# A side step that copies a convolution's or projection's result takes the next step into its unit, and a chunk's rows of B are loaded six units sooner

## The chip, the cores and the metric

The kernel runs on one core of one Trainium2 chip. The metric is the device time of one execution in microseconds (us). The engines are named as in the profile: PE is TensorE's matmul and PEld its weight load, DVE is VectorE, ACT is ScalarE, POOL is GpSimd, and SP is SyncE, which here only issues DMAs (SPq is its queue).

## The reference

Four layers are applied one after the other to an image batch x of shape (8, 48, 48, 96), each as x = x + ss2d(group_norm(x)). What one layer computes, cut to what matters:

```python
xc, z = split(x @ in_proj_w.T)                    # 192 channels each
xc = silu(depthwise_conv3x3(xc) + conv_b)
xs = [xc by rows, xc by columns, and both reversed]   # K = 4 ways through L = 2304 places
dts, Bs, Cs = split(einsum('bkdl,kcd->bkcl', xs, x_proj_w))   # rank, 16, 16 rows
delta = softplus(einsum('bkrl,kdr->bkdl', dts, dt_proj_w) + dt_bias)
def step(h, (u, dl, B, C)):                       # scan over l; h is (b, k, 192, 16)
    h = exp(dl * A) * h + (dl * u) * B
    y = sum over the 16 states of h * C
y = sum of the four ways, put back in place, + D * xs
return (layernorm(y) * silu(z)) @ out_proj_w.T
```

The fourth layer writes the same scan as cumulative sums.

## The kernel before, in words

The images are worked on in four pairs. For each layer and pair, the 192 channels of two images are three tiles t of 128 partitions (the first 128 channels of each image, and the last 64 of both). Each tile is scanned in two orders (ph, by rows or by columns) and two directions (d): 12 groups. A group is three chunks of 768 places, and a chunk has 16 units, n = 0 to 15, each of which holds two of the 16 states for 64 channels. So a pair has 12 x 3 x 16 = 576 units, and layers 0 to 2 have 12 pairs and 6912 units. (Layer 3 runs a short form, "Edge", which the change leaves as it is; a full form of layer 3 stands behind a condition.)

The order of all work is written out by hand: one Python loop in `run` issues unit after unit, and each engine then works through its own queue in that order. In iteration k, which scans unit k, the loop issues:

1. loads by SP (`get_ready`): `load_b` the rows of B, spread over 64 partitions, for the pooled unit k+5 (tile `bb`, line L740), `load` those of C for unit k+4 (tile `cb`, L740). At the first unit of a chunk `load` also loads `brow` (L765): the chunk's rows of B for all states, as three bf16 parts on 96 partitions, in two DMAs. It has two buffers. As `load` runs four units ahead, this is issued at n = 12 of the chunk before;
2. `spread` of unit k+1: for 10 of 16 units PE multiplies `brow` by a 0/1 matrix `pick` and so spreads two rows over a PSUM tile `b` (L678; two buffers). For the six pooled units (n = 2, 5, 7, 10, 13, 15) ACT writes the decay exp(dl*A) into such a tile instead (L780);
3. `weigh` of unit k+3 if pooled: POOL multiplies `bb` by du (L757), and `decay` by ACT (L780);
4. the carries (ACT, L698), and `scan`: DVE multiplies `b` by du (L810, not for pooled units) and scans (L814); POOL multiplies C by the result (L823);
5. one step of `prepare` for the next chunk (delta and delta * u; lines L614 to L645, L589);
6. one side step through `beside`, not at n = 3, 9 and 10 (`full`);
7. `add_up` of unit k-2: PE adds the products up over the states (L870);
8. at n = 12 and 14 (`free`) a second side step.

Side steps belong to two generators that run beside a pair: `behind`, the epilogue of the pair before (layernorm, gate, output projection, residual; L1031 to L1136), and `ahead`, the prologue of the pair that follows (group norm, in-projection L411 and L420 with copies L415 and L424, convolution L314 with its copy L322, x_projections L472 with copies L483 and L485, and the splitting of B into bf16 parts). For the first pair a third, `rest`, finishes its own prologue. `side_step` takes the side that holds a PSUM bank, or else the one that is less far along by `made / total`. Nearly every step is one visit to one engine: a yield of True says that a bank is filled and must be read next. Both the side steps and `prepare` take their banks from one pool `ps` of two PSUM buffers (`bank()`). A convolution's piece of 480 places is nine steps on PE and then one on ACT, the copy; an in-projection's is one on PE and one on ACT; an x_projection's two on PE and one on ACT. A prologue that waits for buffers of u yields GATED.

Of the kernel before, what the change touches and what calls it, by code (L numbers as in the profile page):

```python
# [40 lines left out]
BF16 = mybir.dt.bfloat16  # L41
# [62 lines left out]
def ss2d_layers_kernel(ctx: ExitStack, tc: tile.TileContext, x_in, consts, weights, out):  # L104
# [177 lines left out]

    GATED, READY = "gated", "ready"
    halves_of = [slice(64 * g, 64 * g + 64) for g in range(2)]

    def prologue(l, p, short=False, first=False):
# [14 lines left out]
        def convolve(pad, t):  # L303

            while place["tiles"] < t and not first:
                yield GATED
            u[t] = upool.tile([P, L], F32, name=f"u_{l}_{p}_{t}", tag="u")
            for c0, m in CHUNKS:
                r0, nr = c0 // W, m // W
                ps = bank()  # L310
                for j in range(9):
                    dy, dx = divmod(j, 3)
                    for half in halves_of:
                        nc.tensor.matmul(  # L314
                            ps[half, :m],
                            ly.diag[:, int(t == 2), j, half],
                            pad[:, r0 + dy : r0 + dy + nr, dx : dx + W],
                            start=(j == 0),
                            stop=(j == 8),
                        )  # L320
                    yield True
                nc.scalar.activation(  # L322
                    u[t][:, c0 : c0 + m], ps[:, :m], AF.Identity, bias=ly.column(t, C_CONVB)
                )
                yield
            silu(u[t], u[t])
            yield

# [5 lines left out]
        for b in range(2):  # L334
            x = tmp.tile([DM, L], F32, name=f"x_{l}_{p}_{b}", tag="tmp")
            if l == 0:
                loaded = []

                def load(c0, m):
                    ld = sm2.tile([P, 4, DM], F32, name="ld", tag="ld")  # L340
                    nc.sync.dma_start(
                        ld[: m // 4],
                        x_in[2 * p + b, c0 : c0 + m, :].rearrange("(q j) c -> q j c", j=4),
                    )
                    loaded.append(ld)

                load(*CHUNKS[0])
                load(*CHUNKS[1])
                for _ in range(3):
                    yield  # L350
                for i, (c0, m) in enumerate(CHUNKS):
                    q, ld = m // 4, loaded[i]
                    ps = bank()
                    for j in range(4):
                        nc.tensor.transpose(
                            ps[0:DM, j * q : (j + 1) * q], ld[:q, j, :], ident[:q, :q]
                        )
                    yield True
                    nc.scalar.copy(
                        x[:, c0 : c0 + m].rearrange("c (q j) -> c j q", j=4),  # L360
                        ps[0:DM, :m].rearrange("c (j q) -> c j q", j=4),
                    )
                    if i + 2 < NCH:
                        load(*CHUNKS[i + 2])
                    yield
            for c0, m in CHUNKS:
                piece = slice(c0, c0 + m)
                if l == 0:
                    nc.sync.dma_start(src[b, :, piece], x[:, piece])
                else:  # L370
                    nc.sync.dma_start(x[:, piece], src[b, :, piece])
                yield
            for _ in range(2):
                yield


            st = sm1.tile([DM, NCH, 6], F32, name="st", tag="st")
            for i, (c0, m) in enumerate(CHUNKS):
                nc.vector.bn_stats(st[:, i, :], x[:, c0 : c0 + m])
                if i % 2 == 1:  # L380
                    yield
            mv = sm1.tile([DM, 2], F32, name="mv", tag="mv")
            nc.vector.bn_aggr(mv, st.rearrange("p a b -> p (a b)"))
            yield
            ps = bank()
            nc.tensor.matmul(ps[0:DM, 0:1], minus_group, mv[:, 0:1], start=True, stop=True)
            yield True
            mg = sm1.tile([DM, 1], F32, name="mg", tag="mg")
            nc.scalar.copy(mg, ps[0:DM, 0:1])
            dv = sm1.tile([DM, 1], F32, name="dv", tag="dv")  # L390
            nc.scalar.activation(dv, mv[:, 0:1], AF.Square, bias=mg)
            nc.scalar.activation(dv, dv, AF.Identity, bias=mv[:, 1:2])
            yield
            ps = bank()
            nc.tensor.matmul(ps[0:DM, 0:1], group_w, dv, start=True, stop=True)
            yield True
            scale, shift = gn[:, b, 0:1], gn[:, b, 1:2]
            nc.scalar.activation(scale, ps[0:DM, 0:1], AF.Ln, bias=gn_eps[0:DM])
            nc.scalar.activation(scale, scale, AF.Exp, scale=-0.5)
            nc.scalar.activation(shift, mg, AF.Copy, scale=scale)  # L400
            nc.scalar.activation(x, x, AF.Identity, bias=shift, scale=scale)
            yield

            pad = padded(f"pad_{l}_{p}_{b}")
            q0 = 64 * b
            for c0, m in CHUNKS:
                r0, nr = c0 // W, m // W
                rows = slice(1 + r0, 1 + r0 + nr)
                ps = bank()
                for half in halves_of:  # L410
                    nc.tensor.matmul(  # L411
                        ps[half, :m], ly.inw[:, half], x[:, c0 : c0 + m], start=True, stop=True
                    )
                yield True
                nc.scalar.copy(  # L415
                    pad[:, rows, 1 : W + 1], ps[:, :m].rearrange("p (r w) -> p r w", w=W)
                )
                yield
                ps = bank()
                nc.tensor.matmul(  # L420
                    ps[q0 : q0 + 64, :m], ly.inw[:, P:DIN], x[:, c0 : c0 + m], start=True, stop=True
                )
                yield True
                nc.scalar.copy(  # L424
                    pad2[q0 : q0 + 64, rows, 1 : W + 1],
                    ps[q0 : q0 + 64, :m].rearrange("p (r w) -> p r w", w=W),
                )
                yield
            if not (first and b == 1):
                yield from convolve(pad, b)  # L430
        yield from convolve(pad2, 2)
# [42 lines left out]
        def x_projection(i, ph, b):  # L474
# [20 lines left out]
            for j, (c0, m) in enumerate(CHUNKS):  # L495
                later(o + 3 * j, True, mul, 0, c0, m)
                later(o + 3 * j + 1, True, mul, 1, c0, m)
                later(o + 3 * j + 2, False, lambda *a: put(got["ps"], *a), c0, m)
            def store(c0, m):
                nc.sync.dma_start(xd[ph, b, :, c0 : c0 + m], got["xt"][:, c0 : c0 + m])  # L500

# [48 lines left out]
        def x_projections(*which):  # L550
            for i, (ph, b) in enumerate(which):
                (x_projection_of_ends if short else x_projection)(i, ph, b)
            for i in range(max(steps) + 1):
                held = False
                for holds, f, args in steps.get(i, ()):
                    f(*args)
                    held = held or holds
                yield held
            steps.clear()

# [139 lines left out]
    class Chunk:  # L700
# [52 lines left out]
        def weigh(self, n):  # L753

            if self.pooled(n):
                b = self.b[n][:, : self.m]
                nc.gpsimd.tensor_mul(b, b, self.du[n % 2])  # L757

        def load(self, n):

            s, m, at = state[self.l, self.p], self.m, slice(self.c0, self.c0 + self.m)
            if n == 0:
                self.brow = rpool.tile([2 * NR, SCAN], BF16, name="brow", tag="brow")
                for j, b in enumerate(range(2) if self.t == 2 else (self.t, self.t)):
                    nc.sync.dma_start(  # L765
                        self.brow[NR * j : NR * j + NR, :m],
                        s["xb"][self.ph, b, :, self.d, :, at],
                    )
            self.cb[n] = cb = cbpool.tile([P, SCAN], F32, name="cb", tag="cb")
            self.fetch(cb, NS, n)  # L770

# [390 lines left out]
    def side_step(*sides):  # L1162

        for s in sorted(sides, key=lambda s: (not s.held, s.made / s.total)):
            got = next(s.g, s)
            s.held = got is True
            if got is not s and got is not GATED:
                s.made += 1
                return True
        return False  # L1170

    marks = []
# [20 lines left out]
    def run(pairs, short):  # L1193
# [58 lines left out]
        for k, ((l, p, unit), c, n) in enumerate(todo):  # L1252
# [15 lines left out]
            if n == max(0, per - 1 - DECAYS):  # L1268
                while coming_to < len(chunks) and not chunks[coming_to].ready:
                    next(coming)  # L1270
            if n == 10 and coming_to + 1 < len(chunks):
                z = chunks[coming_to + 1]
                if (z.l, z.p) == (l, p):
# [13 lines left out]

            def beside(some):
                for _ in range(some):
                    side_step(rest) or side_step(behind, ahead)  # L1290

            step(coming)
            if l not in short:
# [1 line left out]
            if k >= LAG:  # L1295
# [3 lines left out]
                sum_of(b, bn)  # L1299
                if k > LAG and todo[k - LAG - 1][0][:2] != (bl, bp):  # L1300
                    done = todo[k - LAG - 1][0][:2]
            beside(10 if l in short else n in free)
        for i in range(len(todo) - LAG, len(todo)):
            collected()
            sum_of(todo[i][1], todo[i][2])
# [113 lines left out]
```

## Time and profile before

| | us |
|---|---|
| median of 3 runs (lowest, highest) | 20198.45 (20187.92, 20203.4) |
| the profiled execution | 20189.92 |
| its span, first to last instruction | 20188.1 |
| mean granted TensorE clock in it | 0.913 of full speed |

The costliest groups of the profile (line, engine, operation, tiles and shapes, count, then busy us and mean ns of one, and behind the bar the idle time of the engine just before them with what ended most of it):

```profile
L823 POOL TENSOR_TENSOR cb<-cb,da 128x768 f32<-128x768 f32 x4320 | 7833.8, 1819 | 641.4 <-issue 128.5
L870 PE MATMUL acc<-cb,twin 128*64 128x384 f32 x27648 | 7063.6, 540 | 428.6 <-POOL cb L823 407.7
L814 DVE TENSOR_TENSOR_SCAN da<-da,carry,b 128x768 f32<-128x768 f32 x2880 | 5222.7, 1813 | 177.5 <-ACT carry L698 1.9
L810 DVE TENSOR_TENSOR b<-du,b 128x768 f32<-128x768 f32 x4320 | 4079.2, 944 | 679.1 <-PE b L678 667.7
L780 ACT ACTIVATE da<-dl,a 128x768 f32<-128x768 f32 x4320 | 4016.5, 931 | 440.8 <-POOL cb L823 408.7
```

From one L814 scan to the next, over the 6912 of the main stage, takes 2.62 us on average; a pair takes 1490.4 to 1532.9 us, and a chunk 39 to 49 us by its place in the pair.

### The profile page before, as it was taken

The page shows a single profiled execution, that of the slowest core. Times are in us where ns is not written, and L with a number is a line of the kernel's source. Part 1 is how long each engine was busy: PE and PEld are TensorE (multiplying, and loading weights), DVE is VectorE, ACT ScalarE, POOL GpSimd, SP SyncE. Part 2 cuts the span into 40 slices and gives each one's busy share as a digit, 9 for nine tenths or more (in the row PEclk, how much of TensorE's full clock was granted, in tenths as well). Part 3 has the DMA queues.
Part 4 walks back from the last instruction along what each step waited for, and adds up shares of the span by engine and source line. Part 5 has one row for each costly group of instructions (what it writes and reads, how often), then busy time and mean ns, then how long its engine had stood idle before and what let it go on. Part 6 is the DMA issues. An engine that isn't in the chain of part 4 may idle for free.

```text
span 20188.1 us, 315179 instructions
## 1 busy us (share of the span) xinstructions
PE 16706.7 (83%) x92962; PEld 7669.4 (38%) x92962; DVE 17650.0 (87%) x14161; ACT 16275.9 (81%) x30014; POOL 17759.8 (88%) x10121
## 2 busy tenths in 40 slices
PE   8887887887888888888887888888888887888886
PEld 3333333333333333333333333333333333334555
DVE  6999988998999999999999999999999999996553
ACT  6777887887887887887887887887887887887786
POOL 6999999999999999999999999999999999995442
PEclk9998998998998998998998998998998998999997
DMA  5888888888888898888888888888888888884221
GB/s 159 228 228 221 226 218 221 229 219 222 224 226 224 222 232 222 222 233 222 222 233 221 223 226 223 220 226 223 221 228 221 223 228 222 222 220 117 79 76 51
DMA packets 2021152, 4200.81 MB, mean 208 GB/s; under 512 B 375920, under 2 KB 789360, under 8 KB 2017904
## 3 DMA queue, kind: packets, MB, share of 16 engines
q1 hardware_dynamic: 2019440, 4180.55, 79.9%
q8 instruction: 762, 12.48, 0.3%
q14 instruction: 950, 7.78, 0.2%
HBM read 4026.64 MB, written 152.27 MB: 207 GB/s over the span
## 4 chain that ended last, share of the span: by engine, by line
PE 17%; ACT 16%; DMA 15%; DVE 14%; issue 9%; SPq 3%; POOL 2%; DVEq 0%; ACTq 0%; POOLq 0%
DVE da L814 7%; DMA cb<-xd 6%; DMA bb<-xd 5%; PE acc L870 4%; DVE b L810 4%; ACT b L780 3%; PE ps L634 2%; PE ps L314 2%; ACT dl L589 2%; ACT du L589 2%; ACT da L780 2%; SPq L740 2%; PE b L678 2%; DVE bb L814 2%; DMA brow<-xb 2%
## 5 line engine op out<-in xcount | busy, mean ns | idle before, releaser
L823 POOL TENSOR_TENSOR cb<-cb,da 128x768 f32<-128x768 f32 x4320 | 7833.8, 1819 | 641.4 <-issue 128.5
L870 PE MATMUL acc<-cb,twin 128*64 128x384 f32 x27648 | 7063.6, 540 | 428.6 <-POOL cb L823 407.7
L814 DVE TENSOR_TENSOR_SCAN da<-da,carry,b 128x768 f32<-128x768 f32 x2880 | 5222.7, 1813 | 177.5 <-ACT carry L698 1.9
L757 POOL TENSOR_TENSOR bb<-bb,du 128x768 f32<-128x768 f32 x2592 | 4715.9, 1819 | 386.3 <-DMA bb<-xd 221.1
L823 POOL TENSOR_TENSOR cb<-cb,bb 128x768 f32<-128x768 f32 x2592 | 4712.7, 1818 | 54.3 <-DVE bb L814 31.8
L810 DVE TENSOR_TENSOR b<-du,b 128x768 f32<-128x768 f32 x4320 | 4079.2, 944 | 679.1 <-PE b L678 667.7
L780 ACT ACTIVATE da<-dl,a 128x768 f32<-128x768 f32 x4320 | 4016.5, 931 | 440.8 <-POOL cb L823 408.7
L678 PE MATMUL b<-brow,pick 96*64 96x512 bf16 (+2 forms) x18816 | 2837.9, 349 | 1545.8 <-DVE da L814 1123.2
L870 PEld LDWEIGHTS acc<-cb,twin 128*64 128x64 f32 x27648 | 2355.2, 148 | 3536.3 <-issue 2177.9
L780 ACT ACTIVATE b<-dl,a 128x768 f32<-128x768 f32 x2592 | 2337.4, 902 | 1115.8 <-DVE da L814 1015.7
L814 DVE TENSOR_TENSOR_SCAN bb<-b,carry,bb 128x768 f32<-128x768 f32 x1728 | 3109.7, 1800 | 94.0 <-ACT b L780 66.8
L814 DVE TENSOR_TENSOR_SCAN da<-da,b 128x768 f32<-128x768 f32 x1440 | 2524.6, 1753 | 87.4 <-DVE b L810 0.9
L678 PEld LDWEIGHTS <-pick 96*64 96x64 bf16 x18816 | 1149.4, 116 | 3794.4 <-DVE da L814 2251.3
L314 PE MATMUL ps<-pad,diag 128*64 128x480 f32 (+1 forms) x8640 | 2169.2, 563 | 69.8 <-DVE eyc L1086 32.5
L589 ACT COPY du<-ps 64x384 f32<-64x384 f32 x3456 | 1635.7, 473 | 236.7 <-DVE ps L645 118.6
L589 ACT COPY dl<-ps 64x384 f32<-64x384 f32 x3456 | 1634.3, 473 | 212.3 <-PE ps L634 171.4
L634 PE MATMUL ps<-du,cst 128*64 128x384 f32 (+1 forms) x7296 | 1581.4, 501 | 259.4 <-ACT du L628 244.8
L814 DVE TENSOR_TENSOR_SCAN bb<-b,bb 128x768 f32<-128x768 f32 x864 | 1502.1, 1739 | 151.8 <-ACT b L780 108.8
L634 PE MATMUL ps<-dl,cst 128*64 128x384 f32 (+1 forms) x7296 | 1453.9, 486 | 0.0
L614 PE MATMUL ps<-dts,w 6*128 6x384 f32 (+5 forms) x2432 | 920.7, 578 | 391.2 <-ACT du L589 214.6
L314 PEld LDWEIGHTS ps<-pad,diag 128*64 128x64 f32 x8640 | 665.1, 138 | 769.6 <-issue 571.4
L634 PEld LDWEIGHTS ps<-du,cst 128*64 128x64 f32 x7296 | 621.1, 142 | 871.1 <-ACT du L628 452.9
(144 smaller groups left out, 19011.3 us busy)
## 6 DMA issues: line engine op xcount, KB each, us to landing
cb<-xd SPq DMA_DIRECT2D x13952, 192.0 KB
bb<-xd SPq DMA_DIRECT2D x5184, 192.0 KB
brow<-xb SPq DMA_DIRECT2D x864, 72.0 KB
ey<-yd SPq DMA_DIRECT2D x256, 216.0 KB
cb<-xd SPq DMA_DIRECT2D x128, 384.0 KB
yd<-y SPq DMA_DIRECT2D x216, 192.0 KB
ex<-xs SPq DMA_DIRECT2D x256, 108.0 KB
xb<-parts SPq DMA_DIRECT2D x96, 216.0 KB
```

The costliest lines, as they stand in the source:

```text
L314: nc.tensor.matmul(ps[half, :m], ly.diag[:, int(t == 2), j, half], pad[:, r0 + dy : r0 + dy + nr, dx : dx + W], start=(j == 0), stop=(j == 8),
L589: nc.scalar.copy(z[64 * h : 64 * h + 64, g, at], v[64 * g : 64 * g + 64])
L614: nc.tensor.matmul(o[:, :m], ly.dtw[q0 : q0 + r, k, chans], dts[q0 : q0 + r, at], start=True, stop=True,)
L634: nc.tensor.matmul(v[half], ident[:, half], z1, start=(i == 0), stop=(i == 3))
L678: nc.tensor.matmul(o[64 * h : 64 * h + 64], pick[:, b, n : n + 1].to_broadcast([2 * NR, 64]), rows, start=True, stop=True,)
L740: nc.sync.dma_start(o[64 * h : 64 * h + 64, : self.m], xd[self.ph, b, row : row + 1, self.c0 : self.c0 + self.m].to_broadcast([64, self.m]),)
L757: nc.gpsimd.tensor_mul(b, b, self.du[n % 2])
L780: nc.scalar.activation(da, self.dl[n % 2], AF.Exp, scale=layers[self.l].a2[:, int(self.t == 2), n % 2, k, i : i + 1],)
L810: nc.vector.tensor_mul(b, self.du[n % 2], b)
L814: nc.vector.tensor_tensor_scan(way(h), way(da), way(b), start, ALU.mult, ALU.add)
L823: nc.gpsimd.tensor_mul(c, c, h)
L870: nc.tensor.matmul(self.acc[64 * g : 64 * g + 64, a, : self.m // 2], twin, c[:, a, :], start=False, stop=(pair + 2 == NS and not self.turns),)
```

## The change

It has four edits, all of which act in the stage of layers 0 to 2:

- A step that copies a convolution's, in-projection's or x_projection's result out of its bank, with another piece to follow, yields MORE. `side_step` hands this on, and `beside` then makes one more side step in the same unit. That next step is chosen as any other is, so it may be the other generator's.
- The second side step at n = 12 and 14 is made only if `in_arrears()`: if the steps made of both sides lag behind the unit's share of their total, counted one chunk ahead.
- A step of `x_projections` that holds both a copy and other functions passes MORE on, unless one of them holds a bank.
- `brow` of the next chunk is loaded by a new `load_rows` at n = 6, ahead of that iteration's loads, if that chunk is of the same layer and pair; `load` at n = 0 of a chunk loads it only where this was not done.

```diff
-                yield
+                yield MORE if c0 + m < L else None          # convolve, after the copy
...
-                yield
+                yield MORE                                  # in-projection, first copy
...
-                yield
+                yield MORE if c0 + m < L else None          # in-projection, second copy
...
-                later(o + 3 * j + 2, False, lambda *a: put(got["ps"], *a), c0, m)
+                later(
+                    o + 3 * j + 2, MORE if j + 1 < NCH else False,
+                    lambda *a: put(got["ps"], *a), c0, m,
+                )
...
-                    held = held or holds
+                    held = True if held is True else holds or held
...
+        def load_rows(self):
+            if self.brow is not None:
+                return
+            self.brow = rpool.tile([2 * NR, SCAN], BF16, name="brow", tag="brow")
+            for j, b in enumerate(range(2) if self.t == 2 else (self.t, self.t)):
+                nc.sync.dma_start(
+                    self.brow[NR * j : NR * j + NR, : self.m],
+                    state[self.l, self.p]["xb"][
+                        self.ph, b, :, self.d, :, self.c0 : self.c0 + self.m
+                    ],
+                )
...
             if n == 0:
-                self.brow = rpool.tile([2 * NR, SCAN], BF16, name="brow", tag="brow")
...
+                self.load_rows()
...
-                return True
+                return MORE if got is MORE else True        # side_step
...
+            if n == 6 and coming_to < len(chunks):
+                z = chunks[coming_to]
+                if (z.l, z.p) == (l, p) and l not in short:
+                    z.load_rows()
...
             def beside(some):
                 for _ in range(some):
-                    side_step(rest) or side_step(behind, ahead)
+                    if (side_step(rest) or side_step(behind, ahead)) is MORE and l not in short:
+                        side_step(rest) or side_step(behind, ahead)
+
+            def in_arrears():
+                made, total = behind.made + ahead.made, behind.total + ahead.total
+                return made * all_units < total * (unit + NS)
...
-            beside(10 if l in short else n in free)
+            beside(10 if l in short else n in free and in_arrears())
```

More of the change, by code (lines that the diff above doesn't have):

```diff
@@ L281, in ss2d_layers_kernel @@
     place = {"tiles": 3}
-    GATED, READY = "gated", "ready"
+    GATED, READY, MORE = "gated", "ready", "more"
     halves_of = [slice(64 * g, 64 * g + 64) for g in range(2)]
@@ L757, in weigh @@
                 nc.gpsimd.tensor_mul(b, b, self.du[n % 2])
+        def load_rows(self):
[9 more added lines that the diff above has]
+                )
         def load(self, n):
-            s, m, at = state[self.l, self.p], self.m, slice(self.c0, self.c0 + self.m)
             if n == 0:
-                self.brow = rpool.tile([2 * NR, SCAN], BF16, name="brow", tag="brow")
[L764 to L768, printed above, removed]
+                self.load_rows()
             self.cb[n] = cb = cbpool.tile([P, SCAN], F32, name="cb", tag="cb")
```

## The prediction

> **What bounds the kernel now.** I read the page's busy shares first, then one table of windows, then the waits of each engine, and last the timeline at one chunk's edge.
>
> ```profile
> PE 16706.7 (83%) x92962; PEld 7669.4 (38%) x92962; DVE 17650.0 (87%) x14161; ACT 16275.9 (81%) x30014; POOL 17759.8 (88%) x10121
> ```
>
> ```profile
> 171.90:18292.40 18120.50, 15031.71 (x81614) 6533.92 (x81614) 16738.18 (x12599) 14767.95 (x27219) 17043.80 (x9679) 0.91 0.87 224
> 18292.40:20188.10 1895.70, 1551.98 (x10816) 1088.04 (x10816) 901.15 (x1539) 1434.45 (x2667) 710.11 (x425) 0.90 0.26 72
> ```
>
> The first line is the busy time of each engine. The two others are windows: the scan stage of layers 0 to 2 (its columns are PE, PEld, DVE, ACT, POOL, clock, DMA share, GB/s), and the rest. The diff touches the first alone, apart from one wording that changes nothing in the rest. There POOL works 17043.80 of 18120.50 us, DVE 16738.18, and the DMA engines 0.87. So no engine is bound by itself: POOL's idle 1077 us is all that scheduling could ever give, and a delay on PE costs time only when DVE or POOL runs dry behind it. The waits say when that happens:
>
> ```profile
> PE b L678 <- DVE da L814: 1123.2, 1068, 4.3
> ...
> PE b L678 <- DMA brow<-xb: 284.4, 121, 7.5
> ...
> PE ps L420 <- ACT pad L415: 17.9, 19, 1.6
> ...
> DVE b L810 <- PE b L678: 667.7, 522, 12.4
> ...
> POOL bb L757 <- DMA bb<-xd: 221.1, 197, 5.0
> ...
> SPq L740 <- PE b L678: 1377.4, 1181, 7.9
> SPq L740 <- PE acc L870: 1352.8, 1108, 9.2
> ...
> SPq L740 <- DMA brow<-xb: 471.6, 488, 2.0
> ```
>
> Columns: total us, times, longest. PE, about to spread a chunk's first state over the partitions, waits 121 times for the chunk's rows of B (brow); DVE's largest wait is for those spreads. SyncE mostly waits for buffers, so it reaches its loads ahead of time. One edge, in the timeline (start us, duration, engine, in brackets the idle time before):
>
> ```profile
> 3003.74 1.55 SPq L765 DMA_DIRECT2D brow<-xb  x2
> ...
> 3006.64 1.17 SPq L740 DMA_DIRECT2D bb<-xd  x2
> ...
> 3011.04 0.52 PE L678 MATMUL b<-brow,pick 96*64 96x512 bf16 x4 [2.33 <-DMA brow<-xb]
> ...
> 3014.28 1.81 POOL L757 TENSOR_TENSOR bb<-bb,du 128x768 f32<-128x768 f32 x1 [1.35 <-DMA bb<-xd]
> ...
> 3016.67 0.96 DVE L810 TENSOR_TENSOR b<-du,b 128x768 f32<-128x768 f32 x1 [2.27 <-PE b L678]
> ```
>
> brow is issued at 3003.74 and ends PE's wait at 3011.04, 7.3 us later. Behind the waiting spread stand PE's side step and sums, so the next spread is late and DVE idles 2.27. The load of bb, issued just after brow, is late too.
>
> **Part 1, brow six units sooner.** From every brow issue to the scan it feeds I find a median of 10.2 us; in the waiting chunks, from issue to the end of PE's wait, 5.7 to 8.5 us (5th to 95th percentile; median 7.2). Six units of 2.62 us put 15.7 us in front: every such wait goes, except at a pair's first chunk, which is not moved (1 of the 121 waits). What a wait costs: from the scan two units before a chunk to the one four units after it, inside pairs, takes 17.0 us in the 120 chunks with it and 15.57 in the 300 without. Some of this is place, since waits crowd in certain chunks; with the chunk's place in its pair held fixed it is 1.02 us a chunk, or 0.64 us per us of PE's wait. So 120 x 1.02 = 122 us. Lower end: the extra POOL idle of those chunks, 0.63 x 120 = 76. Upper: 1.43 x 120 = 172. I take 122, as it compares like with like.
>
> A page of the Trainium skill speaks against there being anything to gain: "DMA: Bandwidth & Descriptors", Anatomy of one DMA, gives a fixed 2.0 us plus bytes at 436 GB/s (measured on the POOL path). An estimate from it for two loads of 72 KB is 2.3 us, so a load issued 10 us ahead would always be in time, this part would be worth 0, and the sum below would be -18 instead of -140. The trace's 7.2 us, with the DMA engines 0.87 busy, decides against it.
>
> brow's two DMAs are also moved on SP's queue: past six units of cb and bb loads and the load of dts. They take 2 x 0.74 us to issue, and SP waits 471.6 us in all for brow's semaphore. Before, the bb of unit n = 2 came next but one behind them. POOL's waits for a bb that end by that DMA are 119 us where unit 2 is weighed, 18 of them at pair starts, and 39 where unit 7 is. If unit 2 becomes like 7 in-pair, POOL gets 62; unit 13 now comes behind brow (two units behind, not one; its wait is 0.04 a chunk today), and I give it half of that. 31 left; the edges are those where PE waited too, so I count 25 (bounds: a loss of 30 if unit 13 takes it all and more, a gain of 80).
>
> **Part 2, the copy and the next step in one unit, and the second step of n = 12 and 14 only in arrears.** The instructions are the same ones; their place changes. Counted over the 12 pairs: 6024 side steps before, 6014 after (the rest is drained at pair ends); units 12 and 14 with two steps fall from 797 to 301; 552 steps follow a copy in its unit (216 the copy of an in-projection, 188 of an x_projection, 148 of a convolution); 204 of the 552 are the epilogue's step, as the side less far along is taken. Nothing is added to PE, ACT or DVE, so the price is only waits.
>
> Gain: fewer doubled units just before a chunk's edge. In the 300 in-pair chunks without a brow wait, DVE still waits 28 + 110 + 60 = 198 us for spreads at n = 0, 1 and 3. If a quarter of that comes of the doubled units, of which 62% go: 198 x 0.25 x 0.62 = 31. Bounds 0 and 123 (all of it).
>
> Loss: the two banks of `ps`. A step that starts in the copy's own unit finds its bank just being read, and PE's in-order queue (behind it the sums L870 and the next spread, for which DVE waits) stands until ACT has copied. In the instruction streams, of 1495 starts of a bank by a side step, 471 wait for an ACT instruction issued in the same unit; after, 704: 233 more. Nearest row: PE L420 on the copy L415, 17.9 us in 19 waits; about 35 of those starts wait for the copy in their own unit, so 0.51 us each. 233 x 0.51 = 119 us on PE; at most the 0.64 of part 1 reaches the end, 76; a sum stands between and pooled units need no spread, so half: 38. Bounds: 0 (the wait falls where PE waits for DVE anyway, the 1123 us row) and 76.
>
> "Perfetto Trace Analysis", Matmuls, says that independent groups should rotate over PSUM banks so that one's evacuation overlaps the next one's matmuls. Taken alone it speaks against this part: with every added same-unit wait at the full 0.94 us of the L420 row and all on the path, the term would be 219 and the sum a loss of 41.
>
> **Sum.** -122 - 25 - 31 + 38 = -140 us. The profiled execution took 20189.92 (span 20188.1), the median of three is 20198.45, 8.5 above it. 20198.45 - 140 = 20058. With all bounds at their best: -172 - 80 - 123 = -375; at their worst: -76 + 30 + 76 = +30. About 0.2%, 40 us, is what a measurement of this kernel can tell from no change.
>
> **Rivals.**
> 1. Same: the wait moves. PE's next limit at the edge is the release of a spread's buffer (1123 us, 1068 times), and only POOL's 76 us come free, less the loss of 38 to 76: 0 to -38, some 20180. For it: POOL and DVE are both within 8% of full, so freed time on one meets the other. Against: both idle at the same edges.
> 2. Slower: PE stands behind ACT. Place: the 552 followed copies. ACT is 81% busy and its copy queues behind exps of 0.93 us, so a follower may wait a whole copy. Price: at the 0.94 us of the L420 row and 0.64 to the path, 552 x 0.94 x 0.64 = 332, less the 178 gained: +154, 20352. It decides from 0.50 us per follower. For: in-projection and x_projection stretches get up to 18 to 20 steps a chunk instead of 15. Against: L472's and L314's waits for their copies today are a few us in all.
> 3. More gain: the edges' waits hang together, and brow, bb and the remaining spreads go at once: -375 + 38 = -337, 19861.
> 4. The load is not sooner in fact: SP stands at that place for buffers. SP's waits are 1.2 us on average, against 15.7; I give it no share of its own.
>
> **How the numbers follow.** Forecast (-140, its own range 19960 to 20160): 0.55. Rival 3: 0.12. Rival 1, within 40 us: 0.13. Rival 2: 0.20. So faster 0.67, same 0.13, slower 0.20. The range runs from 19900, inside rival 3, to 20250, into the mild half of rival 2; about 0.05 is left out below, 0.14 above.
>
> **What would show it.** PE's wait for brow falls from 284 us to under 30 (pair starts), POOL's for bb from 221 to under 180; DVE's wait L810 for the spread from 668 to about 500; SP's wait for brow stays. PE's waits for the copies (the L420, L472, L314 and first epilogue rows) grow by about 120. The stage 171.90:18292.40 shortens by 140, the tail by nothing. I am wrong if brow's wait is gone and DVE's wait for PE is not smaller (rival 1 or 2), and rival 2 holds if those copy rows grow by over 270.

## The result, and the profile after

The changed kernel takes 20304.74 us, the median of 6 runs (20279.07 to 20316.65), against 20200.93 for 6 runs of the kernel before (20187.92 to 20207.37): a ratio of 1.0051, 95% interval [1.0038, 1.0064]. It is slower by half a per cent, where 140 us less were forecast. The profiled execution took 20299.78 us, at a granted clock of 0.91 of full speed.

First the page: the busy time of each engine.

```profile
span 20297.8 us, 315609 instructions
PE 16716.1 (82%) x92962; PEld 7597.4 (37%) x92962; DVE 17657.5 (87%) x14161; ACT 16272.2 (80%) x30014; POOL 17764.8 (88%) x10121
```

Counts are those of before and no engine works more than 10 us longer, so the 110 us of longer span are all waiting. The windows of the scan stage and of what follows it (PE, PEld, DVE, ACT, POOL busy, clock, DMA share, GB/s):

```profile
172.06:18392.39 18220.33, 15030.23 (x81614) 6454.01 (x81614) 16745.23 (x12599) 14764.96 (x27219) 17048.76 (x9679) 0.91 0.86 223
18392.39:20297.80 1905.41, 1562.44 (x10816) 1095.76 (x10816) 901.60 (x1539) 1433.80 (x2667) 710.16 (x425) 0.89 0.25 71
```

The stage is 18220.33 - 18120.50 = 100 us longer, the rest 10. POOL's work in the stage is within 5 us of before (17048.76 against 17043.80); only its idle time grew. Now the waits (total us, times, longest):

```profile
PE b L682 <- DVE da L825: 1362.9, 1097, 4.3
...
DVE b L821 <- PE b L682: 707.0, 546, 14.1
...
POOL bb L761 <- DMA bb<-xd: 169.7, 125, 5.6
...
PE ps L421 <- ACT pad L416: 54.7, 38, 2.5
...
PE ps L473 <- ACT xt L486: 35.5, 20, 3.4
...
PE ps L315 <- ACT u L323: 33.2, 26, 1.9
...
PE ps L473 <- ACT xt L484: 27.0, 23, 1.7
```

```profile
SPq L744 <- PE acc L881: 1519.3, 1162, 8.0
...
SPq L744 <- DMA brow<-xb: 232.1, 281, 2.0
```

PE's wait for brow, 284.4 us before, no longer appears. In its place the wait for a free spread buffer grew from 1123.2 to 1362.9. DVE's wait for the spreads, the row that the forecast wanted to shrink to 500, is 707.0 against 667.7. And the four rows in which PE waits for a copy that may now be followed add up to 150.4 us, where before they were 33.5 (17.9, 6.7, 3.0 and 5.9, from the trace's records). The timeline shows one such place (start us, duration, engine; in brackets the idle time before):

```profile
4924.27 0.56 ACT L416 COPY pad<-ps 128x480 f32<-128x480 f32 x1
...
4924.88 0.78 PE L1042 MATMUL ps<-ey,centre 128*128 128x144 f32 x2 [1.52 <-ACT pad L416]
...
4927.03 1.52 PE L881 MATMUL acc<-cb,twin 128*64 128x384 f32 x4
...
4928.37 0.51 PE L682 MATMUL b<-brow,pick 96*64 96x512 bf16 x4
...
4928.92 0.96 DVE L821 TENSOR_TENSOR b<-du,b 128x768 f32<-128x768 f32 x1 [3.15 <-PE b L682]
```

This is iteration n = 6 of a chunk. ACT comes to the in-projection's copy late, the epilogue's step L1042 that follows it holds PE for 1.52 us, the sums and the spread of unit 8 stand behind it, and DVE idles 3.15 us. DVE's waits for spreads in the stage, summed by unit from the trace's records, show where this gathers (g1 and g2 are experiments below; us):

| spread of unit | 0 | 1 | 3 | 8 |
|---|---|---|---|---|
| before | 96 | 293 | 108 | 68 |
| early rows alone (e1) | 36 | 211 | 149 | 62 |
| after | 42 | 213 | 96 | 187 |
| after, followers of n = 6 behind the sums (g1) | 49 | 218 | 90 | 145 |
| after, all followers behind the sums (g2) | 33 | 222 | 101 | 122 |

The first two columns carry the gain of the early rows, the last a loss of 119 us. Unit 14, not in the table, goes the same way: 8 us before and in e1, 56 after. Of waits over 1.2 us at unit 8, 24 stand less than 5 us behind a PE wait of over 0.6 us for a copy of the followed kinds: 72 us in all. Before there are none.

### The profile page after: what moved, and what is told of

Read it like the earlier page. It is cut to its first block, busy times and chain, and to the rows that moved or that the text cites. A ratio compares the mean times of both kernels' runs of the same rounds, so it can differ in the third digit from the quotient of the medians.

```text
span 20297.8 us, 315609 instructions
## 1 busy us (share of the span) xinstructions
PE 16716.1 (82%) x92962; PEld 7597.4 (37%) x92962; DVE 17657.5 (87%) x14161; ACT 16272.2 (80%) x30014; POOL 17764.8 (88%) x10121
## 4 chain that ended last, share of the span: by engine, by line
ACT 23%; PE 22%; DVE 20%; DMA 16%; issue 14%; POOL 3%; SPq 3%; DVEq 0%; ACTq 0%; POOLq 0%
DVE da L825 10%; DMA cb<-xd 7%; DMA bb<-xd 6%; DVE b L821 6%; PE acc L881 5%; ACT b L791 4%; ACT dl L593 4%; ACT du L593 3%; PE ps L315 3%; ACT da L791 3%; PE ps L638 3%; DVE bb L825 2%; POOL cb L834 2%; PE b L682 2%; SPq L744 2%
## 5 line engine op out<-in xcount | busy, mean ns | idle before, releaser
L881 PE MATMUL acc<-cb,twin 128*64 128x384 f32 x27648 | 6915.3, 540 | 402.5 <-POOL cb L834 384.2
L821 DVE TENSOR_TENSOR b<-du,b 128x768 f32<-128x768 f32 x4320 | 4081.0, 945 | 722.8 <-PE b L682 707.0
L682 PE MATMUL b<-brow,pick 96*64 96x512 bf16 (+2 forms) x18816 | 2786.9, 349 | 1534.1 <-DVE da L825 1362.9
L881 PEld LDWEIGHTS acc<-cb,twin 128*64 128x64 f32 x27648 | 2285.7, 148 | 3534.7 <-issue 2279.9
L315 PEld LDWEIGHTS ps<-pad,diag 128*64 128x64 f32 x8640 | 622.7, 140 | 837.8 <-issue 554.9
```

What stands on the lines that cost most here:

```text
L315: nc.tensor.matmul(ps[half, :m], ly.diag[:, int(t == 2), j, half], pad[:, r0 + dy : r0 + dy + nr, dx : dx + W], start=(j == 0), stop=(j == 8),
L682: nc.tensor.matmul(o[64 * h : 64 * h + 64], pick[:, b, n : n + 1].to_broadcast([2 * NR, 64]), rows, start=True, stop=True,)
L821: nc.vector.tensor_mul(b, self.du[n % 2], b)
L881: nc.tensor.matmul(self.acc[64 * g : 64 * g + 64, a, : self.m // 2], twin, c[:, a, :], start=False, stop=(pair + 2 == NS and not self.turns),)
```

## The experiments

All are timed over five rounds beside the kernel before on the same chip; differences are against that chip's own median, which lay between 20163 and 20181. Three causes of loss are held against each other, where letters stand for them: W, PE's wait for the bank that is just being copied; D, a second step at a place in the chunk where PE has no room; P, the turn that all later steps are pushed into, so that they meet other units.

**The parts apart.** e1 keeps the early rows alone:

```diff
-                    if (side_step(rest) or side_step(behind, ahead)) is MORE and l not in short:
-                        side_step(rest) or side_step(behind, ahead)
+                    side_step(rest) or side_step(behind, ahead)
-            beside(10 if l in short else n in free and in_arrears())
+            beside(10 if l in short else n in free)
```

e2 is the change without the early rows (the block `if n == 6 ...: z.load_rows()` taken out). e3 is e2 with `n in free` again unconditional, so the followers alone. e4 is e2 without the follower, so the rule `in_arrears` alone.

> The early load of brow alone; the side steps as before. Theory A (the load gains as reckoned, and the followed copies cost more than that): 20200 less 76 to 172, so 20030 to 20125, and PE's wait for brow is gone. Theory B (PE's wait for brow was hidden: another wait takes its place, and the load is worth nothing): within 40 of 20200. Theory C (the load does the harm, by its place in SP's queue ahead of the cb and bb loads of the later half of the chunk): about 20300, with POOL's waits for bb or cb larger than before.

> The other part alone: the followed copies and the second steps of n = 12 and 14 only in arrears; brow is loaded as before. Theory A: 20380 to 20480, that is the changed kernel's 20304 and the load's gain on top. Theory B: about 20305, as the changed kernel. Theory C: about 20200 or below.

> The followed copies alone: second steps at n = 12 and 14 always, as before, brow as before. Theory A1 (a step that starts in its copy's unit holds PE): as slow as the two together, 20380 to 20480. Theory A2 (the loss comes of the second steps that are left out at n = 12 and 14, so that side work runs on longer): near 20200, and the fourth kernel of this set is the slow one.

> The rule of arrears alone: a second step at n = 12 and 14 only where the sides lag; no copy is followed, brow as before. Theory A1: 20170 to 20230, since the steps need nearly all slots without the followers. Theory A2: 20300 or slower.

| | median us (before 20169.88) | ratio [95%] |
|---|---|---|
| e1, rows | 20086.71 | 0.9957 [0.9943, 0.997] |
| e2, followers and arrears | 20389.69 | 1.0107 [1.0091, 1.0122] |
| e3, followers | 20406.04 | 1.012 [1.0104, 1.0135] |
| e4, arrears | 20190.08 | 1.0011 [1.0002, 1.002] |

The parts have opposite signs: -83 us for the rows, +236 for the followers, +20 for the arrears rule. Added to the followers, that rule takes nothing back that can be told from none (e2 is 16 under e3, inside the intervals). All four came as theories A and A1 said. The rows alone are the fastest of all the kernels here that compute the reference's result. The waits of e1:

```profile
PE b L682 <- DVE da L825: 1284.0, 1202, 4.3
...
DVE b L821 <- PE b L682: 559.1, 446, 13.4
...
POOL bb L761 <- DMA bb<-xd: 148.4, 118, 4.5
```

No brow row here either; 161 of the 284 us went over to the buffer's release, and DVE's wait fell by 109.

**Which followers, and W against the rest.** e5, e6 and e7 are e3 with MORE left only in the in-projection (216 followers), the x_projections (188) or the convolution (148). e8 is e3 with every follower issued behind its unit's sums; no step changes its unit:

```diff
-                        side_step(rest) or side_step(behind, ahead)
+                        follow += 1              # beside, which returns it
...
                 sum_of(b, bn)
...
+            beside(follow)
```

> Only the in-projection's copies are followed by another step in their unit (216 of the 552), brow and the second steps of n = 12 and 14 as before. All 552 together cost 236 us (ratio 1.012). If each follower costs the same: +92 us, 0.46%. Theory W (the follower waits for the bank that is being copied, and PE stands): at least its share, since one matmul and one copy alternate here and each start finds a copy just issued: 100 to 160. Theory D (two steps' work in one unit is too much for PE and ACT): most of the loss too, since these stretches get 20 steps a chunk for 15: 120 to 180.

> Only the x_projections' copies are followed (188 of 552). Evenly spread: +80 us. Theory W: 60 to 100; before, a start there waits for an ACT instruction of its own unit in about a quarter of the cases, and with the followers in nearly two thirds. Theory D: 30 to 60, 18 steps a chunk for 15.

> Only the convolution's copies are followed (148 of 552). Evenly spread: +63 us. Theory W: 30 to 70. Theory D: within 20 of nothing, since these stretches keep 15 to 16 steps a chunk.

> All 552 followers, but issued behind the unit's sums (L870 of before) instead of ahead of them, so that the sums no longer stand behind a waiting matmul on PE; the next unit's spread still does. Theory W: the loss of 236 us falls to half or less, and POOL's waits for the sums to free a buffer fall. Theory D: the same work in the same unit, so 200 to 260 as before.

| | median us (before 20180.97) | ratio [95%] |
|---|---|---|
| e5, in-projection | 20325.05 | 1.0073 [1.0059, 1.0087] |
| e6, x_projections | 20229.22 | 1.0025 [1.0015, 1.0034] |
| e7, convolution | 20395.98 | 1.0102 [1.0087, 1.0118] |
| e8, all, behind the sums | 20334.87 | 1.0074 [1.006, 1.0088] |

The kinds don't add: 144 + 48 + 215 = 407 us, all together 236. A price for each follower can't do that; a shift of the order of all that comes later can. The price isn't the same either: 0.67 us for an in-projection's follower, 0.26 for an x_projection's, 1.45 for a convolution's. e5 lies in the ranges of both theories, e6 in D's, e7 far above both (W said at most 70, D 20), and e8 between its two.

In e8 82 of 236 us came back, a third of the loss. Not all of it need be W: the time of the followers' own matmuls stands behind the sums now too, and the edit doesn't part the two. Nor need it be all of W, as PE's waits for ACT at the matmuls that write `ps` show. They are of two kinds, those of the side steps and those of `prepare`, which takes its banks from the same two (us in the stage, summed from the records; s2, f1, f2 and g2 are described below):

| | side steps | `prepare` | both | time against before |
|---|---|---|---|---|
| before | 304 | 463 | 767 | |
| e4, arrears | 434 | 338 | 772 | +20 |
| e3, followers | 616 | 293 | 909 | +236 |
| e8, behind the sums | 487 | 298 | 785 | +154 |
| s2, lead 6 | 427 | 497 | 924 | +126 |
| f1, second steps at 5 and 7 | 385 | 288 | 673 | +246 |
| f2, one unit after the copy | 414 | 412 | 826 | +106 |
| e1, rows | 311 | 486 | 796 | -83 |
| after | 547 | 369 | 916 | +104 |
| g2, after, behind the sums | 438 | 386 | 824 | +42 |

Both kinds together are in e8 nearly back at before's, and the time is still 154 us over. But the side steps alone still wait 183 us more than before; e8 took away only 129 of their 312. If all 312 cost what these 129 did, 0.64 us each, W would be 198 of the 236. e4 speaks against that price, as its 130 us more of side steps' waits, with 126 less of `prepare`'s, cost only 20. So W's share of the loss isn't shown; a third is what this edit took back. f1 fits no such price: 81 us more and 246 us lost. And s2 and f2, in which no copy is followed, have 123 and 110 us more of the same waits: a changed turn makes some by itself.

**Order without any follower.** s2 and s6 are the kernel before with two or six more empty steps ahead of the epilogue:

```diff
-        for _ in range(4):
+        for _ in range(6):          # s6: range(10)
             yield
```

d1 is before, and d2 is e3, with `silu(ps, ps)` in the epilogue replaced by `nc.scalar.copy(ps, ps)`.

> The kernel before with one number changed: the epilogue's generator begins with six empty steps for four. No copy is followed and no work is added; every epilogue step, and what takes turns with it, only meets another unit of the chunk. Theory P (what the followers change is mainly where the heavy steps fall: ACT's silu of the epilogue with its two table loads, and DVE's multiply behind it): 20100 to 20400, off from 20180 by 40 us or more in either direction. Theory W (the loss is the followers' own wait for a bank just being copied): within 25 us of 20180.

> The same with ten empty steps for four. Theory P: off by 40 us or more, and not by the same amount as with six; 27 of the epilogue's silus then fall on n = 7, where ACT has the twin copies to make, for 16 before, so slower. Theory W: within 25 us of 20180.

> The kernel before with the epilogue's silu left out: a copy of the same tile in its place, so that its two table loads of 1.28 us each are gone and its result is not the reference's. It is the base for the next kernel. Table loads of 192 epilogue pieces in the stage are 493 us of ACT's time; I expect 19850 to 20050.

> The followed copies alone (as the kernel that lost 236 us) with the same silu left out. Against the kernel just before: theory P says that most of the 236 us go with the heavy step, 0 to 90 are left. Theory W says that the waits for banks stay: 190 to 260 are left.

| | median us (before 20169.09) | ratio [95%] |
|---|---|---|
| s2, lead 6 | 20295.12 | 1.0067 [1.0054, 1.0081] |
| s6, lead 10 | 20264.67 | 1.0049 [1.0035, 1.0062] |
| d1 | 19841.19 | 0.9837 [0.9824, 0.9851] |
| d2 | 20034.35 | 0.9933 [0.992, 0.9947] |

Two empty steps, which issue nothing, cost 126 us, more than the whole change; they only let the epilogue's steps meet other units. 46 of the 126 lie behind the scan stage, where this lead counts too, but the stage itself is 42 longer, and with six steps 64 (28 behind it); those are profiled runs and need not add up to the medians' difference. Both shifts came as P said and not as W did, though s6 was expected to be the slower of the two. Each made the time longer, so before's order is a favourable one as far as these two show. The silu isn't the main cause: without it the followers still cost 20034.35 - 19841.19 = 193 us, inside W's 190 to 260 and not P's 0 to 90. So P, if it holds, doesn't work through this heavy step.

**Place and turn.** f1 is before with the second step at other units and no follower; f2 lets the convolution's first PE step of the next piece take the second along, one unit after the copy (the copy isn't followed); f3 lets the convolution's copy be followed always by its own next step; f4 is e7 with the epilogue's lead raised to 6. f2 and f3 stand on e7 too, so all three have neither the early rows nor the arrears rule.

```diff
-    full, free = (3, 9, 10), (12, 14)
+    full, free = (3, 9, 10), (5, 7)                 # f1
...
-                    yield True
+                    yield TWICE if j == 0 < c0 else True     # f2, and a plain yield after the copy
...
-                        side_step(rest) or side_step(behind, ahead)
+                        side_step(last_side[0])     # f3, with MORE in the convolution alone
```

> The kernel before with the second side steps at n = 5 and 7 for 12 and 14: as many doubled units (806 for 797), no copy followed. Theory D (a second step costs by the unit it falls in: 12 and 14 have room, the others do not): 20300 to 20450, +0.6% or more. If only the turn of the heavy steps counts (theory P, as two shifts of the epilogue have shown 96 and 126 us of the median): about 20280, like these. Theory W (waiting for banks just being copied): within 25 us of 20175.

> As many followers as in the convolution's kernel (148), from the same generator, but one unit later: the first step of a convolution's next piece takes the second step with it, and the copy is followed by nothing. The bank was copied a unit ago, so nothing waits for it. Theory W: near 20175 to 20230, the 206 us mostly gone. Theory D and P: 20280 to 20400.

> The convolution's copies followed, but always by the convolution's own next step, where 88 of 148 were the epilogue's. Theory W: the most waits for the bank just copied, 20380 to 20450. Theory D and P: as the kernel of this set with the followers one unit later, within 40 us of it, 20280 to 20400.

> The convolution's copies followed as in the kernel that lost 206 us, and the epilogue's start shifted by two empty steps. Theory P (much of the 206 us is the turn in which heavy steps meet units): off from 20390 by 40 us or more, likely down, as two steps shifted up without followers cost 126. Theory D and W: the followers cost what they cost, 20390 plus the shift's own 50 to 126, so 20430 to 20510.

| | median us (before 20168.08) | ratio [95%] |
|---|---|---|
| f1 | 20414.59 | 1.0125 [1.0111, 1.014] |
| f2 | 20274.45 | 1.0057 [1.0045, 1.0069] |
| f3 | 20312.1 | 1.0074 [1.0061, 1.0087] |
| f4 | 20261.22 | 1.0052 [1.0039, 1.0065] |

f1 doubles 806 units, before 797; its PE waits of `ps` for ACT fall from 767 to 673 us; still it costs 246, the largest loss of all. Its spreads and its products come later:

```profile
L823 POOL TENSOR_TENSOR cb<-cb,da 128x768 f32<-128x768 f32 x4320 | 7835.3, 1819 | 797.2 <-issue 184.0
...
L810 DVE TENSOR_TENSOR b<-du,b 128x768 f32<-128x768 f32 x4320 | 4083.4, 945 | 735.5 <-PE b L678 726.6
```

The figures behind the bar, idle time, were 641.4 and 679.1 before; the work is the same. So where a second step stands sets a price, of its own or by the turn of what follows; f1 doesn't part D from P. f3 less f2, 38 us over 148 followers or 0.25 each, is what comes of the copy's bank with about the same pacing (the two intervals overlap); the other 106 of 144 come with no copy followed. W had f3 dearer than e7; it is 71 us cheaper. f4 is 100 to 120 us under e7 (by the ratios and by the medians' distances to their own before): the lead that cost 126 us in the kernel before gains about as much here. A fixed price for a follower or a doubled unit can't have both signs; a turn can.

**W in the changed kernel itself.** g1 is the changed kernel with the 48 followers of n = 6 issued behind the sums, g2 with all 552, by the edit of e8. Every step stays in its unit.

> The changed kernel, with one difference: of the 552 steps that follow a copy, the 48 of unit n = 6 are issued behind that unit's sums (L881) instead of ahead of them. Every step stays in its unit. In the trace of the changed kernel 24 waits of DVE for the spread of n = 8, 72 us in all, stand behind a wait of PE for a copy that was followed; the kernel before has none there. Theory (the followed copy holds PE at this place): DVE's waits for the spread of n = 8 fall from 187 us to about 115, and the time falls by 40 to 72 us, to 20235 to 20265 on the scale of a before of 20200, a ratio of 1.002 to 1.003. Rival (the units in which the steps lie, not the wait): the wait comes back two or three units later and the time stays within 20 us of the changed kernel, 1.004 to 1.006.

> The changed kernel with all 552 followers issued behind the sums of their unit. Theory: the early rows' gain of 85 us stays, the followers' waits for a bank just being copied go (86 us came back in the same edit without the early rows and the arrears rule, and this kernel has more of them at n = 6): 85 to 120 us less than the changed kernel, a ratio of 0.999 to 1.001. Rival (place and turn of the steps set the loss): 30 us less at most, 1.004.

| | median us (before 20163.44) | ratio [95%] |
|---|---|---|
| g1 | 20258.58 | 1.0044 [1.003, 1.0058] |
| g2 | 20205.92 | 1.002 [1.0011, 1.0029] |

g1 decides little. DVE's wait at unit 8 fell by 42 of the 72 us, and its wait for spreads in all by 34, from 707.0 to 672.7. 0.0007 of the ratio came back, 14 us with an error of some 40 by the two intervals. That is under the theory's 40 to 72 and inside the rival's 20, but whether the 42 us were lost again elsewhere can't be told. g2 took 0.0031, 62 us, between its two expectations. Its waits:

```profile
DVE b L821 <- PE b L682: 624.0, 522, 14.1
```

```profile
PE ps L421 <- ACT pad L416: 35.9, 34, 1.8
...
PE ps L473 <- ACT xt L486: 21.4, 21, 1.4
...
PE ps L315 <- ACT u L323: 19.3, 26, 1.3
...
PE ps L473 <- ACT xt L484: 13.0, 17, 1.0
```

These copy rows fell from 150.4 to 89.6 us, 61 less, and the time by 62; as all waits of side steps for ACT fell by 109 (547 to 438), that is not a price of one for one. Yet g2 is still 127 us above e1 (0.0063 of the ratio), which has the same early rows.

## Why the prediction was wrong

**The early rows: right mechanism, too large.** The step said -122 for brow and -25 for bb; e1 measured -83. The load was late, and PE's wait for brow went with it entirely. But 1.02 us a chunk took a chunk without the wait as the model of one freed from it. The freed one met the next limit, the buffer's release, with 161 of the 284 us, as rival 1 had described it. The bb term had both its parts too small, and they nearly cancel: POOL's wait for the late bb fell at n = 15 (unit 2 weighed) from 119 to 8 us, where 62 were counted, and rose at n = 10 (unit 13 weighed, now behind brow) from 7 to 80, where 31 were, so 38 us were left for 31. The 62 rested on a wrong reading: in the records none of unit 2's 119 us stands at a pair's first chunk, where the step has 18, but 27 of unit 7's 39 do. What bb's part was worth in time, no run parts from brow's. The estimate from the Trainium skill's page "DMA: Bandwidth & Descriptors", Anatomy of one DMA, 2.3 us for the loads by a fit of the POOL path, left nothing to gain here; e1's 83 us decide against it for SP's loads among this traffic.

SP's wait for brow didn't stay: 471.6 to 232.1 us, with the wait for the sums' buffer up from 1352.8 to 1519.3 in the changed kernel. No term of the sum rested on it.

**The steps: the term that failed.** Part 2 was put at +38 - 31 = +7 us. Measured, it is +220 alone (e2 less before, 20389.69 - 20169.88) and 0.0094 of the ratio, 190 us, on top of e1. Three things went wrong, from small to large:

- The gain of 31 for fewer doubled units isn't there: the rule alone makes +20 (e4), and DVE's waits for the spreads of units 0, 1 and 3 did not fall with it: 532 us in e4, 497 before. So the doubled units 12 and 14 weren't what made them.
- W was underpriced. On the rows that were named, PE's waits for the copies were to grow by about 120 us and grew by 116 (54 to 170, from the records); over all matmuls into `ps` by 166 (85 to 251), and the side steps' waits for any ACT instruction by 243 (304 to 547). I let half of what reached the end fall away, 38 with a bound of 76; g2 got 62 back by removing only part of them. f3 less f2, e8 and g2 put a quarter to 35% of the loss on the followers' place at the bank and ahead of the sums (38 of 144, 82 of 236, 62 of 190). If the rest of the waits is as dear as the part removed, it depends on what is counted. With `prepare`'s waits (767 before, 916 after, 824 in g2) it would be 62 x 149/92 = 100 us here in all, about half; with the side steps' alone, 62 x 243/109 = 138.
- What lacked altogether was the price of moving steps. The text said that the instructions were the same, only in another place, "so the price is only waits", and then counted only one kind of wait, on the bank. Every follower puts a step into a unit whose PE time was laid out for one, and shifts all later steps. Bounds of 0 to 76 us were those of the wait alone. Without followers f1 lost 246 us, with only 81 us more of side steps' waits for ACT, and s2 and s6, which shift steps only, 126 and 96 (42 and 64 of them in the stage, by the profiled runs).

So rival 2 came in its direction, near its price before the gain (236 measured alone, 332 written) but not by its mechanism: it was to hold if the copy rows grew by over 270 us, and they grew by 116 on the rows named. Only the waits of side steps for any ACT instruction come near, with 243.

The Trainium skill's page "Perfetto Trace Analysis", Matmuls, named a true cost, the step that finds its bank still being read. Its term of 219 us lies near the followers' 236 and its sum, a loss of 41, nearer than mine; as the runs took only a third of the 236 back at the bank and don't show the rest to be its, the nearness may be luck.

What stays open: how W, D and P share the 190 us. 62 came back with the followers behind the sums; 52 to 128 are left by the counts above for D and P, and through which waits these work isn't shown. The losses of f1 and s2 spread over many rows, and no run moved a step without moving those behind it. Part of it may be the clock, of which below.

## What to carry to other kernels

When a hand-written order feeds in-order queues, an edit that makes the same instructions come in another unit can have a price of its own, of either sign, that no wait of the old trace shows; here two empty steps cost more than the whole change. Price such an edit with a dummy first: two empty steps in one generator tell how much the present order is worth, and no forecast of a reordering should be surer than that figure. An edit that only issues a load earlier leaves the order of the engines alone and can be forecast from its wait, less what the next limit takes (here over half).

## What was not expected of the hardware

- Two empty steps, which issue nothing, moved the time by 0.67% [0.54, 0.81], about half of it behind the scan stage by the profiled run.
- The granted clock goes with the order of the same work: mean of the timed runs 0.916 in e1, 0.912 to 0.913 before, 0.911 after, 0.906 in e2, 0.899 in f1. Among runs of one kernel 0.01 less clock goes with 67 us more (regression over 172 runs, each about its kernel's mean). If that is what the clock costs, it carries some 36 of the 190 us between e1 and after, and 90 of f1's 246. Which of the two leads the other isn't shown.
- The sum of a kind of wait over the stage can hide its parts: with the arrears rule alone PE's waits for ACT at `ps` stay as they were (767 and 772 us), while 130 us go over from `prepare` to the side steps, and the time grows by 20.
